# A three-layer CIN on one core: VectorE makes X_1 ahead of T3_1 in the second pairs, chunk 4's factor moves behind T3_0, the first pairs' squarings behind a copy

## The chip, the cores and the metric

The kernel runs on one core of a Trainium2 chip. Its time is in device microseconds (us), the median of three runs. A profile is one execution, taken by the hardware profiler; its times count from the span's start. Engines: PE (TensorE), with its weight loads as PEld; DVE (VectorE); ACT (ScalarE); POOL (GpSimd); SP, which issues loads.

## The reference

A compressed interaction network over `x` of shape 1024 x 64 x 16 (rows, fields f, elements e), all in float32:

```python
x0 = x; h = x
for i in range(3):
    z = einsum('bfe,bge->bfge', x0, h).reshape(B, 64 * 64, 16)
    y = einsum('oc,bce->boe', W[i], z) + b[i][None, :, None]     # W[i]: 128 x 4096
    x_i, h = (y[:, :64], y[:, 64:]) if i < 2 else (y, y)
    xs.append(x_i)
out = sum(concatenate(xs, axis=1), axis=2) @ fc_w.T + fc_b        # 1024 x 1
```

Only one number per row leaves it, so the kernel folds the third layer and the sums into products of pairs of fields with small weight matrices made at the start. What is left per row and element is a set of contractions of all products `x_f * x_g`.

## The kernel before

**Chunks and quarters.** The 1024 rows are 32 chunks of 32 rows; a chunk is 512 columns (32 rows x 16 elements). For chunk c, `xa_c` holds `x` on 128 partitions in 4 rotations i, `xb_c_j` holds it in quarter j of 4 further rotations. The product of the two (128 x 4 x 512, a block of 2048 columns) holds a quarter of the field pairs. Fourteen such blocks (`z`) lie in SBUF; `take` and `used` (lines 87 to 96) hand them out in the order in which they come free, worked out when the program is built.

**Pairs.** Chunks 0 to 5 are done singly. Chunks 6 to 31 are done two at a time, as pairs n = 0 to 12 (k = 3 to 15), each of a chunk a and a chunk b. A pair is one 2 x 2 block product done with seven multiplications in place of eight, so that sums of products stand in for some of them. VectorE makes, for j = 0 and 1 (`make_pair`, line 694; `w_product`, line 640):

- B22_j: `xa_b` times quarter j + 2 of b;
- a small sum in place (`w_both`, line 646): quarter j of b is added into the PSUM bank that holds quarter j + 2;
- T3_j: `xa_b` times that sum, from the same PSUM bank;
- X_j: `xa_a` times quarter j of a;
- B21_j: `xa_a` times quarter j + 2 of a.

Each product but T3 has a quarter that ScalarE first copies into a PSUM bank (`second`, line 554); there are two such banks, used in turn. GpSimd then mixes (`w_mix`, line 651): T2 from X and T3, later others; for j = 1 T2 is written over X in place (line 654), in two halves. One mix of each pair is an accumulating DMA.

**TensorE.** It multiplies the products and mixes with weights of 64 columns (`mm`, line 527). Two matmuls lie side by side on the two halves of the array's columns, so that a pair of them goes at a time. Four sums per pair stay in PSUM: alpha, beta, gamma (the other half of alpha's bank) and delta. The banks of alpha and delta come from four banks with the tag `acc`, used in turn; before them the sums of chunks 4 and 5 lie there too, so pair 1's alpha and delta take the banks of chunks 4 and 5.

**Order.** Nothing is scheduled by a planner at run time. Every operation is entered in a list with a time by hand (`at(when, fn, ...)`, line 518). Sorted by that time, the list gives the order of each engine's queue; semaphore waits follow from the data and from the reuse of buffers. A pair's window begins at `t = T0 + 31 * n` (line 914); one unit is two matmuls side by side, about 0.86 us. For pairs 1 and later the ten numbers handed to `make_pair` (line 928) are the times, from t, of B22_0, the sum, T3_0, X_0, B22_1, the sum, T3_1, X_1, B21_0 and B21_1; a quarter's copy is entered 2.7 units ahead of its product (line 709). The next seven are GpSimd's mixes.

In odd pairs (`a_leads`, line 785) the window of TensorE opens with X_1 (into alpha) beside T3_0 and then T3_1 (into delta). In even pairs (`o_leads`, line 798) it opens in another order. Even pairs have `joint` 0 (the last one 2), odd ones 1 (line 909).

**Other parts that the change touches.** `factors(c)` (line 287) closes the single chunks 4 and 5: ScalarE scales half of the chunk's sum (line 291), VectorE multiplies it with the other half (line 298). Chunk 4's is entered at T0 + 11, chunk 5's at T0 + 25.3 (line 900); these times lie in pair 0's window. `square(c)` (line 179) squares a chunk on ScalarE; `load_pair` (line 829) enters the two squarings of a pair 10 units into its window (line 839). `load_pair` also enters the loads on SP: `xa` has three slots, so that a chunk's load waits until the last product that reads the slot's old chunk is done.

Of the kernel before, what the change touches and what calls it, by code (L numbers as in the profile page):

```python
# [70 lines left out]
def cin_kernel(ctx, tc, xra, xrb, wh, w0r, w1h, w2t, wx1, wx0, vec, lin, out):  # L71
# [298 lines left out]
    for h in range(2):  # L370
        at = slice(32 * h, 32 * h + 32)
# [146 lines left out]
    def at(when, fn, *args, **flags):  # L518
        ops.append((when, len(ops), fn, args, flags))
# [174 lines left out]
    def make_pair(t, p, when, mixed):  # L694
        a, b = p["a"], p["b"]
        for when, c, j, name, uses in (
            (when[0], b, 2, "B22", 5), (when[1], b, 0, None, 0), (when[2], b, 0, "T3", 9),
            (when[3], a, 0, "X", 5), (when[4], b, 3, "B22", 5), (when[5], b, 1, None, 0),
            (when[6], b, 1, "T3", 9), (when[7], a, 1, "X", 13 if p["k"] > 3 else 5), (when[8], a, 2, "B21", 5),
            (when[9], a, 3, "B21", 5),  # L700
        ):
            if name is None:
                at(t + when, w_both, p, j)
                continue
            if name == "B21" and j == 2 and p["k"] == 3:
                at(t + when, w_product, p, c, j, name, uses, engine=nc.gpsimd)
                continue
            if name != "T3":
                ahead = 3.3 if p["k"] > 4 and name == "B22" and j == 2 else 2.7
                if p["k"] == 3 and name == "X" and j == 1:  # L710
                    ahead = 9.1
                at(t + when - ahead, second, c, j)
            at(t + when, w_product, p, c, j, name, uses)
        t2, t1, t4 = ("T2", "X", "T3"), ("T3", "B22", "T2"), ("T2", "T2", "B21")
        for when, j, names in zip(
            mixed, (0, 1, 1, 0, 1, 1, 0), (t2, (*t2, 0, 2), (*t2, 2), t1, t1, t4, t4)
        ):
            if names == t4 and j and p["k"] % 2:
                at(t + when - 1.5, w_mix, p, j, *names, 0, 2)
                names = (*t4, 2)  # L720
            at(t + when, w_mix, p, j, *names)
        at(t + 29, lambda: used(p["B21"][p["k"] % 2 ^ 1]))
# [51 lines left out]
    def first_window(t, p, after, left):  # L774
        window(
            t, p,
            p1_run(p, GROUPS) + left[1][:1] + [(q_extra, 4, va)] + w_run(p, alpha, s2, "T2")
            + left[1][1:] + w_run(p, alpha, s1, "T3"),
            p7_run(p, GROUPS) + left[0][:1] + [(q_extra, 5, va)]
            + w_run(p, beta, wq_all, "B21", True, 2 * NI) + left[0][1:]  # L780
            + p1_run(after, FIRST_ROW) + p4_run(p)[:-LATE],
            8, 8, 18,
        )
# [29 lines left out]
    def end_pair(t, p, whens):  # L813
        hb_, qa, uub, ha, uua, xv, add = whens
        at(t + hb_, w_hb, p)
        at(t + qa, w_qa, p)
        at(t + uub, w_uu, p, alpha, "A", snaps[2])
        at(t + ha, w_ha, p)
        at(t + uua, w_uu, p, delta, "O", snaps[0])
        if p["joint"] == 0:  # L820
            at(t + uub - 0.1, w_hb_squares, p)
        if p["joint"] == 1:
            at(t + xv, x_v0x_parts, p)
        else:
            at(t + xv, x_v0x, p["k"])
        at(t + add, sums, p["k"])


    def load_pair(t, p, b0, a0, b1, a1):
        a, b = p["a"], p["b"]  # L830
        at(t + b0, load_xa, b)
        at(t + b0, load_xb, b, 2, 0)
        at(t + a0, load_xa, a)
        at(t + a0, load_xb, a, 0)
        at(t + b1, load_xb, b, 3, 1)
        at(t + a1, load_xb, a, 1, 2, 3)
        for c in (b, a):
            at(t + 1, load_e, c)
            at(t + 10, square, c)
        at(t + 1.1, load_xx, p["k"])  # L840


# [54 lines left out]
    for c in (0, 1):  # L897
        at(34.5, factors, c)
    at(34.6, sums, 0, slice(0, 128), slice(0, 1))
    for c, when in ((4, 11), (5, 25.3)):  # L900
        at(T0 + when, factors, c)
    at(T0 + 29.1, sums, 2, slice(0, 128), slice(0, 1))

# [9 lines left out]
    for n, p in enumerate(pairs):  # L913
        t = T0 + SPAN * n
        q, after = pairs[n - 1], pairs[n + 1] if n + 1 < NPAIR else None
        if n == 0:
            load_pair(t, p, -39.9, -33.3, -39.8, -27)
            make_pair(
                t, p, (-23.4, -20.7, -20.4, -16.5, -17.2, -16.8, -16.6, -7, -13.5, 3),
                (-14, -6.9, -6.8, 7.2, 12.4, 17.6, 15.9),  # L920
            )
            first_window(
                t, p, after, [[(contract_half, 5, 3, i, h) for i in (2, 3)] for h in range(2)]
            )
        else:
            load_pair(t, p, -34, -28, -27.8, -27.7)
            make_pair(
                t, p, (-21.4, -18.7, -18.4, -15.8, -12.2, -9.5, -6.1, -2, 1.6, 4.2),
                (-5, 1.6, 3.6, 7.2 if n % 2 else 0.2, 12.4, 18.6, 18.5 if n % 2 else 16.9),
            )  # L930
            (a_leads if n % 2 else o_leads)(t, p, q, after)
            if n % 2:
                end_pair(t, q, (0.7, 11.7, 21.2, 22.3, 23.2, 21.3, 36))
            else:
                end_pair(t, q, (0.7, 11.7, 17.9, 22.3, 23.2, 17.8, 36))
# [36 lines left out]
    t, q = T0 + SPAN * NPAIR, pairs[-1]  # L972
# [184 lines left out]
```

## Time and profile before

| | us |
|---|---|
| median of three runs (447.61 to 448.14) | 447.92 |
| the profiled execution, its own time | 447.98 |
| its span, first to last instruction | 446.2 |
| TensorE busy | 441.4 |
| VectorE busy | 403.6 |
| GpSimd busy | 367.5 |
| ScalarE busy | 116.9 |
| products at L642 on VectorE, 103 | 231.2, 2.28 each |
| mixes at L659 on GpSimd, 85 | 300.7, 3.57 each (4.55 a whole block, 2.4 a half) |
| windows of pairs 0, 1, 2, 3 begin on TensorE at | 84.3, 109.2, 136.2, 161.2 |

The granted clock of TensorE is 1.00 throughout. The profile's lines hold, for a group of instructions, line, engine, operation, output <- input, count, then busy time and the mean of one in ns, then the idle time before them and what ended most of it. In a timeline a line has start, length, engine, line, operation, and in brackets the idle time before it with the releaser. `PEld alpha L528 <- DVE z L642` in the list of waits reads: a weight load for a matmul into alpha stood until VectorE's product of line 642 was done. Matmul ends are modelled, so idle time of TensorE is read from the starts.

### The profile page before, as it was taken

The page shows a single profiled execution, that of the slowest core. Times are in us where ns is not written, and L with a number is a line of the kernel's source. Part 1 is how long each engine was busy: PE and PEld are TensorE (multiplying, and loading weights), DVE is VectorE, ACT ScalarE, POOL GpSimd, SP SyncE. Part 2 cuts the span into 40 slices and gives each one's busy share as a digit, 9 for nine tenths or more (in the row PEclk, how much of TensorE's full clock was granted, in tenths as well). Part 3 has the DMA queues.
Part 4 walks back from the last instruction along what each step waited for, and adds up shares of the span by engine and source line. Part 5 has one row for each costly group of instructions (what it writes and reads, how often), then busy time and mean ns, then how long its engine had stood idle before and what let it go on. Part 6 is the DMA issues. An engine that isn't in the chain of part 4 may idle for free.

```text
span 446.2 us, 5956 instructions
## 1 busy us (share of the span) xinstructions
PE 441.4 (99%) x2234; PEld 153.4 (34%) x2234; DVE 403.6 (90%) x305; ACT 116.9 (26%) x215; POOL 367.5 (82%) x135
## 2 busy tenths in 40 slices
PE   9999999999999999999999999999999999999997
PEld 5333333334333333333333333333333333333345
DVE  4996899979998999989999999989999899999744
ACT  2263341232313223131312223131231313123211
POOL 5424788998998979899798979989798997989900
PEclk9999999999999999999999999999999999999999
DMA  8997996399649775796929877497747968492400
GB/s 304 414 337 191 374 410 266 86 354 246 258 106 312 207 239 176 169 356 138 325 84 235 295 203 269 115 326 184 255 166 176 352 138 326 129 271 64 95 1 0
DMA packets 35060, 99.85 MB, mean 224 GB/s; under 512 B 6388, under 2 KB 7188, under 8 KB 28440
## 3 DMA queue, kind: packets, MB, share of 16 engines
q1 hardware_dynamic: 31560, 84.70, 54.0%
q0 software_dynamic: 1872, 13.63, 16.7%
q10 hardware_dynamic: 1600, 1.15, 1.1%
q8 instruction: 17, 0.28, 0.3%
q14 instruction: 11, 0.09, 0.1%
HBM read 84.20 MB, written 1.64 MB: 192 GB/s over the span
## 4 chain that ended last, share of the span: by engine, by line
PE 88%; DMA 6%; DVE 4%; issue 1%; ACT 1%; SPq 0%; DVEq 0%
PE alpha L528 40%; PE delta L528 22%; PE beta L528 11%; PE acc L528 6%; PE q L528 3%; DMA xa<-in_xra 3%; PE acc L281 3%; DVE z L642 2%; DMA xb<-in_xrb 2%; PE acc L248 2%; DMA z<-in_w0r 1%; DVE z L240 1%; PE y L528 0%; DVE uu L298 0%; DVE xp L648 0%
## 5 line engine op out<-in xcount | busy, mean ns | idle before, releaser
L659 POOL TENSOR_TENSOR z<-z,z 128x2048 f32<-128x2048 f32 (+1 forms) x85 | 300.7, 3571 | 25.5 <-PE alpha L528 14.8
L642 DVE TENSOR_TENSOR z<-xa,xp 128x2048 f32<-128x2048 f32 x103 | 231.2, 2280 | 3.0 <-ACT xp L556 1.8
L528 PE MATMUL alpha<-z,ws 128*64 128x512 f32 x624 | 233.1, 593 | 0.0
L528 PEld LDWEIGHTS alpha<-z,ws 128*64 128x64 f32 x624 | 72.9, 137 | 91.5 <-issue 86.4
L528 PE MATMUL delta<-z,w_all 128*64 128x512 f32 x208 | 96.4, 592 | 0.0
L528 PE MATMUL alpha<-z,w_all 128*64 128x512 f32 x208 | 92.7, 593 | 1.0 <-DVE z L642 1.0
L528 PE MATMUL beta<-z,w_all 128*64 128x512 f32 x208 | 91.7, 594 | 0.0
L528 PE MATMUL delta<-z,ws 128*64 128x512 f32 x208 | 91.7, 594 | 0.0
L556 ACT COPY xp<-xb 128x512 f32<-128x512 f32 x88 | 51.3, 585 | 134.4 <-DVE z L642 113.4
L240 DVE TENSOR_TENSOR z<-xa,xp 128x2048 f32<-128x2048 f32 (+1 forms) x29 | 45.5, 1620 | 3.6 <-ACT xp L556 2.2
L240 POOL TENSOR_TENSOR z<-xa,xb 128x2048 f32<-128x2048 f32 x6 | 27.3, 4570 | 17.1 <-DMA xb<-in_xrb 17.0
L528 PEld LDWEIGHTS alpha<-z,w_all 128*64 128x64 f32 x208 | 28.0, 137 | 33.3 <-issue 26.0
L528 PEld LDWEIGHTS delta<-z,w_all 128*64 128x64 f32 x208 | 28.5, 137 | 30.4 <-issue 29.7
L528 PEld LDWEIGHTS beta<-z,w_all 128*64 128x64 f32 x208 | 28.0, 137 | 27.4 <-issue 25.7
L528 PEld LDWEIGHTS delta<-z,ws 128*64 128x64 f32 x208 | 28.0, 137 | 27.4 <-issue 25.7
L528 PE MATMUL acc<-z,w_all 128*64 128x512 f32 x128 | 28.1, 592 | 0.0
L673 ACT ACTIVATE snap<-alpha,vs 64x512 f32<-64x512 f32 x13 | 8.9, 682 | 49.8 <-PE alpha L528 49.8
L248 PE MATMUL acc<-z,w_all 128*64 128x512 f32 x96 | 21.6, 598 | 0.3 <-DVE z L240 0.3
L305 DVE TENSOR_REDUCE acc<-uu 128x64 f32<-128x1024 f32 (+2 forms) x19 | 19.6, 1036 | 0.2
L676 ACT COPY snap<-delta 64x512 f32<-64x512 f32 x13 | 7.5, 581 | 42.6 <-PE alpha L528 28.3
L648 DVE TENSOR_TENSOR xp<-xp,xb 128x512 f32<-128x512 f32 x26 | 18.1, 697 | 0.6
L670 ACT COPY snap<-alpha 64x512 f32<-64x512 f32 x13 | 7.6, 581 | 39.9 <-PE delta L528 25.6
(130 smaller groups left out, 369.1 us busy)
## 6 DMA issues: line engine op xcount, KB each, us to landing
xa<-in_xra SPq DMA_DIRECT2D x32, 1024.0 KB, 5.8
xb<-in_xrb SPq DMA_DIRECT2D x128, 256.0 KB, 6.9
z<-z POOLq DMA_DIRECT2D x13, 1024.0 KB, 8.1
e<-in_xra SPq DMA_DIRECT2D x28, 128.0 KB, 7.0
xx<-in_xra SPq DMA_DIRECT2D x28, 128.0 KB, 2.6
z<-in_w2t SPq DMA_DIRECT2D x2, 1024.0 KB, 8.7
z<-in_wx SPq DMA_DIRECT2D x2, 1024.0 KB, 10.4
xa<-in_xra SPq DMA_DIRECT2D x5, 256.0 KB, 4.0
```

The source lines that it names most:

```text
L240: engine.tensor_tensor(blocks[zs[c, j]][:, at, :], xas[c][:, at, :], xbs[c][j].unsqueeze(1).to_broadcast([128, last - first, N]), ALU.mult,)
L248: nc.tensor.matmul(accs[c][halves[i % 2]], w_all[:, j * NI + i, 0:64], blocks[zs[c, j]][:, i, :], start=(j == 0 and i < 2), stop=(j == las ...
L281: nc.tensor.matmul(accs[c][halves[1 - c % 2]], w_all[:, t, 64:128], blocks[zs[c, j]][:, i, :], start=(t == 0), stop=False, skip_group_chec ...
L305: nc.vector.tensor_reduce(acc[rows, of, k, half], uu[rows, of if at is None else at, E * half.start : E * half.stop].rearrange("p k (b e) ...
L528: nc.tensor.matmul(out, w, rhs, start=start, stop=stop, skip_group_check=True)
L556: nc.scalar.copy(bank, xbs[c][j])
L642: engine.tensor_tensor(blocks[b], xas[c], xbs[c][j].unsqueeze(1).to_broadcast([128, NI, N]), ALU.mult)
L648: nc.vector.tensor_tensor(bank, bank, xbs[p["b"]][j], ALU.add)
L659: nc.gpsimd.tensor_tensor(*(blocks[b][:, first:last] for b in (o, x, y)), ALU.subtract if in1 == "T3" else ALU.add,)
L670: nc.scalar.copy(snaps[0][p["O"]], alpha(p))
L673: nc.scalar.activation(snaps[1][p["O"]], alpha(p), AF.Identity, bias=bh1[p["A"]])
L676: nc.scalar.copy(snaps[2][p["A"]], delta(p))
```

## The change

Three times in the list of operations are changed. No operation is added or taken away.

```diff
@@ load_pair @@
         for c in (b, a):
             at(t + 1, load_e, c)
-            at(t + 10, square, c)
+            at(t + (10 if p["joint"] == 1 else 14), square, c)
         at(t + 1.1, load_xx, p["k"])
@@ the single chunks 4 and 5 @@
-    for c, when in ((4, 11), (5, 25.3)):
+    for c, when in ((4, 12.7), (5, 25.3)):
         at(T0 + when, factors, c)
@@ pairs 1 and later @@
             load_pair(t, p, -34, -28, -27.8, -27.7)
             make_pair(
-                t, p, (-21.4, -18.7, -18.4, -15.8, -12.2, -9.5, -6.1, -2, 1.6, 4.2),
+                t, p, (-21.4, -18.7, -18.4, -15.8, -12.2, -9.5, -6.1, -6.2 if n % 2 else -2, 1.6, 4.2),
                 (-5, 1.6, 3.6, 7.2 if n % 2 else 0.2, 12.4, 18.6, 18.5 if n % 2 else 16.9),
             )
```

- In odd pairs ("second pairs") X_1 is entered at -6.2, just ahead of T3_1 at -6.1, instead of -2; its quarter's copy on ScalarE moves with it, to -8.9. On VectorE the two products change places. As blocks are handed out in the order of the list, X_1 and T3_1 also get other blocks than before.
- Chunk 4's factor is entered at T0 + 12.7, which is behind pair 1's T3_0 (T0 + 12.6); its scaling on ScalarE moves with it, behind the copy for pair 1's X_0 (T0 + 12.5).
- In even pairs ("first pairs") the two squarings are entered 14 units into the window instead of 10, behind the copy for the next pair's X_0 (12.5 units in).

Chunk 5's factor keeps its time, T0 + 25.3. That is 5.7 units ahead of pair 1's window: behind T3_1, and before the change ahead of X_1, after it behind X_1.

## The prediction

> **What bounds the kernel now.** I read the shares of busy time first, then the list of waits, then the timelines of the places that the waits point at. The page gives, engine by engine, busy time, share of the span and instructions:
>
> ```profile
> PE 441.4 (99%) x2234; PEld 153.4 (34%) x2234; DVE 403.6 (90%) x305; ACT 116.9 (26%) x215; POOL 367.5 (82%) x135
> ```
>
> TensorE is the bound, so only time in which it stands still can be won. A matmul record of 512 columns is followed by the next one of its column half 0.43 us later, two halves side by side; I looked for larger steps. From 84 us on there are only two kinds: around the matmuls on squares (64 rows; 0.53, 0.48 and 0.54, 0.48 us), which the change leaves alone, and at the start of the odd pairs' windows. The list of waits has the second kind (total, times, longest, in us; two groups of the same wait):
>
> ```profile
> PEld alpha L528 <- DVE z L642: 6.4, 7, 1.8
> ...
> PE alpha L528 <- DVE z L642: 1.0, 1, 1.0
> ```
>
> One is long, six are short. The long one is pair 1's start, in TensorE's timeline:
>
> ```profile
> 107.44 0.59 PE L528 MATMUL delta<-z,w_all 128*64 128x512 f32 x1
> 107.65 0.59 PE L528 MATMUL alpha<-z,ws 128*64 128x512 f32 x1
> 109.20 0.64 PE L528 MATMUL alpha<-z,w_all 128*64 128x512 f32 x1 [0.96 <-DVE z L642]
> ```
>
> The next two matmuls were due at 107.87 and 108.08 and both start at 109.20. What they wait for is in VectorE's timeline:
>
> ```profile
> 103.74 2.29 DVE L642 TENSOR_TENSOR z<-xa,xp 128x2048 f32<-128x2048 f32 x1
> 106.06 0.76 DVE L298 SCALAR_TENSOR_TENSOR uu<-acc,vs,snap 64x512 f32<-64x512 f32 x1
> 106.85 2.29 DVE L642 TENSOR_TENSOR z<-xa,xp 128x2048 f32<-128x2048 f32 x1
> ```
>
> These are T3_1, chunk 5's factor and X_1. X_1 ends at 109.14 and TensorE starts 0.06 later. T3_1, made first, is first read four matmul pairs later, at 112.69. Pair 3's start shows the short kind:
>
> ```profile
> 160.63 0.59 PE L528 MATMUL delta<-z,w_all 128*64 128x512 f32 x1
> 160.64 0.59 PE L528 MATMUL alpha<-z,ws 128*64 128x512 f32 x1
> 161.17 0.64 PE L528 MATMUL alpha<-z,w_all 128*64 128x512 f32 x1
> 161.18 0.64 PE L528 MATMUL delta<-z,ws 128*64 128x512 f32 x1
> 161.65 0.59 PE L528 MATMUL alpha<-z,w_all 128*64 128x512 f32 x1
> ```
>
> A step of 0.54 and one of 0.48 in place of 0.43 each; T3_1 and X_1 lie together on VectorE from 156.63 to 161.12, X_1 last, and TensorE starts 0.05 after it.
>
> **A rule that speaks against a gain here.** The steps at 161 look like those around the squares (123.41 to 123.94, then 0.48), where the tile form goes from 128*64 to 64*64. The Trainium skill, TensorEngine Tiling (Array Packing), Key Properties, says that a change of tiling mode drains TensorE; were the short steps such drains, the 0.81 us below would stay and the sum would be 447.06. The row decides against it: the form is 128*64 on both sides at 161, the even pairs' starts (188.14 to 188.57, 0.43) show no step at the same place, and X_1's end stands 0.05 before the start all five times.
>
> **The change part by part.**
>
> *Pairs 3, 5, 7, 9, 11: X_1 and T3_1 change places on VectorE.* Nothing is added. Both take 2.28, so X_1 ends at 158.92 instead of 161.12 and T3_1 at 161.12. The start is then free: the five steps are 0.541, 0.540, 0.535, 0.544 and 0.541, less 0.429 each: 0.56; the five second steps of 0.48 give 5 x 0.051 = 0.25. Together **0.81 us**. What is late next:
> - T3_1 on TensorE is wanted at 164.66, 3.5 after its end. GpSimd's mix of X_1 and T3_1 starts at 163.18 and is held by TensorE's reading of X_1 (idle 2.65, released by alpha), not by T3_1.
> - The block that T3_1 now takes was last read by GpSimd's half mix that ends at 155.88; VectorE comes at 158.9. Spare: 3.
> - The PSUM bank of T3_1's operand is copied over for the next product (B21_0). That copy started at 158.95, now at 161.15; 0.59 later it is there, at 161.74. VectorE is covered until 162.03 by the sum at L680 (161.28, 0.76). Spare: 0.3, so 0.
> - SP's queue: the load of the next pair's chunk a into the slot that T3_1 read was issued at 158.95, now at 161.15, with six quarter loads behind it. At the medians in this stretch (4.7 us to landing for a chunk, 6.9 for a quarter) the chunk lands at 165.9, its first quarter at 168.5; the readers come at 173.44 (VectorE) and 169.97 (ScalarE). Spare: 1.5 or more, so 0.
> - The next tightest products for TensorE over the whole run have 1.7 us to spare, in the even pairs.
>
> *Pair 1: the same swap, and chunk 4's factor behind T3_0.* Before, VectorE stands 2.55 us idle until 94.69, because the factor waits for ScalarE's scaling (94.06), and that for the two squarings in front of it (92.89 to 94.04). After, step by step from 92.14, where the product before ends: sum 0.70, T3_0 2.28, factor 0.75, X_0 2.28, B22_1 2.28, sum 0.70, with some 0.1 between: 101.2. X_1 then needs its quarter copied by ScalarE, which sits behind the copy at L673 (100.36, 0.68, released by TensorE): ready at 101.65. X_1 runs to 104.0, 4 us before it is due. T3_1 cannot follow at once: its new block is the one that pair 0's B21_1 held (the order of both programs with their waits shows a wait for GpSimd), and GpSimd reads that until the second half of this row:
>
> ```profile
> 100.13 9.57 POOL L659 TENSOR_TENSOR z<-z,z 128x1024 f32<-128x1024 f32 x3
> ```
>
> (two halves, 100.13 to 105.08, and a product). So T3_1 runs 105.15 to 107.43. Chunk 5's factor is queued behind it, and lands at 108.22. **Here a wait is added**: the window's second matmul, the first into delta, writes the PSUM bank that chunk 5's factor reads. Before, the factor was done ahead of X_1, so that the wait for X_1 covered it; in the changed program this matmul waits for VectorE itself. It starts at 108.22 + 0.06 = 108.28 against 108.08 due: 0.20 of stall takes the place of 1.12. Behind it stands all of TensorE's queue, but the other half runs on until its own next matmul at 108.73, as the halves did 0.2 apart before 107.87. Gain **0.92 us**. Bounds: 1.17 if GpSimd's block is free earlier and nothing waits (1.12 and the second step's 0.05); 0, if chunk 5's factor comes as late as X_1 did. I take 0.92, since each duration in it is a row. VectorE then reaches B21_0 at 109.7 instead of 110.56; GpSimd's next mix, which waited 1.51 for TensorE at 111.21, starts at about 109.7.
>
> *The even pairs' squarings, four units later, and chunk 4's scaling on ScalarE.* ScalarE is 26% busy. At 143.86 the two squarings (0.62 each) stand in front of the copy for X_0 (144.91), and X_0 starts at 147.78; the squares are read at 164.65 and later. 0 either way, with 2 us of cover on one side and 19 on the other.
>
> Sum against the profiled execution's own time of 447.98 (span 446.2 and 1.8 around it): 447.98 - 0.81 - 0.92 = 446.25. The median of the runs shown is 447.92, 0.06 lower; by it 446.2. To the end of the kernel nothing takes the gain back: the last window's products have 10 us and more to spare, and TensorE runs without a step from 423 on.
>
> **Rivals.**
> 1. *The short steps stay* (another wait comes within 0.1 of X_1's, or a restart that no row names). Only pair 1 pays: 447.98 - 0.92 = 447.06. For: the steps are small, and I know only that X_1's end fits. Against: no other product ends within 1.7 us.
> 2. *Pair 1's stall only changes its name*: T3_1 is held longer by GpSimd and chunk 5's factor comes at 109.1. Only the odd pairs pay: 447.17. For: VectorE has nothing else to do in that place and GpSimd's spans are rough. Against: GpSimd's chain up to 105.08 is the same program, without idle time.
> 3. *Nothing*: both hold, 447.9. The program does do what it says: in the order of the changed kernel X_1 stands ahead of T3_1 in all six odd pairs.
> 4. *Slower*: B21_0's copy. It can start only when T3_1 ends. Place: VectorE at 162.0 in the six odd pairs. It costs nothing until it is 0.3 late (the sum's cover) and then 1.7 more (the spare of the even pairs' X_1); past 2.0 us each further one costs one, six times. For 0.2% slower, 448.8, it would need (448.8 - 446.25) / 6 = 0.43 past that point; at 0.55 past it, 449.5. Against: ScalarE is idle from 153.99 to 158.95, with nothing ahead of the copy.
>
> **How the numbers follow.** Both gains: 0.71, own range 445.7 (pair 1's 1.17, and 0.3 for the spread of the median; the runs shown lie 0.5 apart) to 446.8. Short steps stay 0.11; pair 1's stall stays 0.08; nothing 0.05; slower 0.05. The range takes in the first two rivals: 445.7 to 447.2, which leaves about 0.1 outside, and spread. Faster than 447.92 by over 0.2% (about what a measurement here can tell from no change) means below 447.02: all of the first, half of rival 1, a third of rival 2: 0.79. Same: the rest of those and rival 3: 0.16. Slower 0.05.
>
> **What would show it.** In the changed kernel's waits, alpha's wait for the product at L642 falls from 6.4 us to the plain 0.3 each; the five starts step by 0.43. At pair 1's start the wait names L298, on delta, and is about 0.2. VectorE's 2.55 idle before L298 is gone, and T3_1 of pair 1 stands idle for GpSimd about 1 us. The starts of pairs 3, 5, 7, 9, 11 come every 51.8 us instead of 51.97. Wrong would be: a step at a pair's start with another releaser, or ScalarE's copies released later than the sum at L680 ends.

## The result, and the profile after

The changed kernel takes 445.48 us (median of 6 runs, 445.25 to 446.4) against 447.97 of the kernel before (6 runs, 447.59 to 448.49): a ratio of 0.9947 [0.9934, 0.996], 2.49 us less. The forecast was 446.2 with a range of 445.7 to 447.2. The sign and both mechanisms were right; the gain was 2.49 in place of 1.73, and the time lies 0.22 below the range.

The profiled execution is the slowest of the six: 446.40, span 444.6, granted clock 1.00. Its own gain, 447.98 - 446.40 = 1.58, is less than forecast. So the profile has to be read with care: it shows what went from pair 1 on, and something else that differs from execution to execution.

The page of the changed kernel, first part:

```profile
PE 440.5 (99%) x2234; PEld 154.0 (35%) x2234; DVE 403.5 (91%) x305; ACT 117.3 (26%) x215; POOL 367.4 (83%) x135
```

TensorE is still the bound. Its list of waits (total, times, longest, in us) has three lines on the products of line 642 and on line 298 that matter here:

```profile
DVE z L642 <- POOL z L659: 1.1, 1, 1.1
...
PEld alpha L528 <- DVE z L642: 0.3, 1, 0.3
...
PEld delta L528 <- DVE uu L298: 0.2, 1, 0.2
```

Alpha's waits for products of line 642 have fallen from 6.4 us in seven times and 1.0 in one to 0.3 in one, and that one stands at 138.39, in pair 2's window, not at an odd pair's start. (Of the seven, six were for X_1; the seventh, 0.45 at 100.73, lay in pair 0's window, so the prediction's "six are short" counts one too many.) What has come instead is the new wait that the forecast named, on delta, for chunk 5's factor. VectorE waits once 1.1 for GpSimd's block. TensorE's timeline at pair 1's start:

```profile
107.83 0.59 PE L528 MATMUL alpha<-z,ws 128*64 128x512 f32 x1
108.05 0.59 PE L528 MATMUL alpha<-z,w_all 128*64 128x512 f32 x1
108.42 0.64 PE L528 MATMUL delta<-z,ws 128*64 128x512 f32 x1
```

X_1 is no longer waited for: alpha starts at 108.05, 0.22 after the matmul before, as the halves did ahead of it. Delta was due 0.21 later, at 108.26, and starts at 108.42. VectorE's timeline says why:

```profile
101.93 2.29 DVE L642 TENSOR_TENSOR z<-xa,xp 128x2048 f32<-128x2048 f32 x1 [0.67 <-ACT xp L556]
105.29 2.29 DVE L642 TENSOR_TENSOR z<-xa,xp 128x2048 f32<-128x2048 f32 x1 [1.07 <-POOL z L659]
107.61 0.76 DVE L298 SCALAR_TENSOR_TENSOR uu<-acc,vs,snap 64x512 f32<-64x512 f32 x1
```

X_1, then T3_1 held by GpSimd, then chunk 5's factor, which ends at 108.37; TensorE follows 0.05 later. GpSimd's timeline shows the two halves and the whole-block mix behind them in one row (the prediction calls the third operation of this row a product; line 659 is a mix):

```profile
100.40 9.34 POOL L659 TENSOR_TENSOR z<-z,z 128x1024 f32<-128x1024 f32 x3
```

The halves end at 105.26, and T3_1 starts 0.03 later. Pair 3's start on TensorE has no short step left (159.85 to 160.28 is 0.43, as everywhere):

```profile
159.85 0.59 PE L528 MATMUL delta<-z,w_all 128*64 128x512 f32 x1
159.86 0.59 PE L528 MATMUL alpha<-z,ws 128*64 128x512 f32 x1
160.28 0.59 PE L528 MATMUL alpha<-z,w_all 128*64 128x512 f32 x1
```

**Where the time went.** I set the starts of the same matmuls of the two profiles against each other, by their place in TensorE's queue. Ahead of pair 1 the changed kernel is 0.18 *later*, from 43 to 101 us and by the same amount throughout. Behind pair 1's start, once the two column halves run level again, it is 0.78 earlier; behind the two steps of the starts of pairs 3 to 11 it is 0.94, 1.10, 1.26, 1.43 and 1.59 earlier, and 1.59 at the end. So the part of the kernel that the change touches won 1.59 + 0.18 = 1.77 us, against a forecast of 1.73, and an unchanged part, ahead of 43 us, lost 0.18. The other five runs must have been earlier in that part, or have won more in the touched one. That is the open question.

### The profile page after: what moved, and what is told of

Same layout as the page of the kernel before. It is cut to its first block, busy times and chain, and to the rows that moved or that the text cites. A ratio compares the mean times of both kernels' runs of the same rounds, so it can differ in the third digit from the quotient of the medians.

```text
span 444.6 us, 5946 instructions
## 1 busy us (share of the span) xinstructions
PE 440.5 (99%) x2234; PEld 154.0 (35%) x2234; DVE 403.5 (91%) x305; ACT 117.3 (26%) x215; POOL 367.4 (83%) x135
## 4 chain that ended last, share of the span: by engine, by line
PE 91%; DMA 6%; DVE 1%; SPq 0%; issue 0%; DVEq 0%
PE alpha L528 42%; PE delta L528 23%; PE beta L528 10%; PE acc L528 7%; PE q L528 3%; DMA xa<-in_xra 3%; PE acc L281 3%; DMA xb<-in_xrb 2%; PE acc L248 2%; DMA z<-in_w0r 1%; DVE z L240 1%; PE y L528 0%; SPq L145 0%; SPq L195 0%; PE hx L528 0%
```

## The experiments

**Theory.** Two separate things were removed: chunk 4's factor behind T3_0 takes away the stall of pair 1, the swap takes away the short steps of pairs 3 to 11. What lies beyond them is scatter of the start-up, and has nothing to do with the change. **Rivals:** the swap alone, or the squarings, did what the factor is credited with; or the changed kernel really starts earlier, by a mechanism that the forecast missed.

For each run two numbers come from the profile: the *start-up*, how much later the matmul that stood at 43.18 in the first profile of before starts, and what was *won* between there and the end. 447.98 plus the first less the second gives every profiled execution's own time within 0.05 us, so what lies outside these two (behind the last matmul, and around the span) hardly varies. In `e3` and `e4` the two column halves stand 0.03 apart at that place; the later one is taken. The names in brackets are those by which the text calls the runs.

| run | median us (runs) | before, beside it | ratio | start-up | won | own time |
|---|---|---|---|---|---|---|
| the changed kernel, first | 445.48 (6) | 447.97 | 0.9947 [0.9934, 0.996] | +0.18 | 1.77 | 446.40 |
| again (`e1_again`) | 445.56 (5) | 447.86 | 0.9948 [0.9936, 0.9961] | -0.75 | 1.98 | 445.25 |
| again (`e6_after`) | 445.88 (5) | 447.79 | 0.9958 [0.9946, 0.9971] | +0.01 | 1.98 | 446.00 |
| again (`e9_after`) | 445.38 (1) | 447.77 | | -0.64 | 1.99 | 445.38 |
| swap only (`e2`) | 446.39 (6) | 447.86 | 0.9967 [0.9955, 0.9979] | +0.33 | 1.17 | 447.18 |
| no swap (`e5`) | 446.56 (7) | 447.86 | 0.9971 [0.996, 0.9982] | 0.00 | 1.21 | 446.80 |
| factor 4 only (`e8`) | 446.83 (11) | 447.79 | 0.9978 [0.9969, 0.9987] | +0.02 | 1.20 | 446.84 |
| squarings only (`e7`) | 447.30 (11) | 447.77 | 0.9993 [0.9984, 1.0002] | -0.20 | 0.52 | 447.27 |
| chunk 5's factor ahead too (`e3`) | 445.87 (5) | 447.86 | 0.9955 [0.9942, 0.9967] | -0.07 | 1.99 | 445.93 |
| swap not in pair 1 (`e4`) | 445.79 (5) | 447.79 | 0.9958 [0.9944, 0.9971] | +0.21 | 1.98 | 446.20 |
| before against itself (`b1`) | 447.91 (11) | 447.79 | 1.0002 [0.9994, 1.0011] | -0.06 | 0.02 | 447.91 |
| before, one profile (`b2`) | 447.92 (1) | 447.77 | | -0.03 | 0.03 | 447.92 |

### The changed kernel again

No edit.

> The changed kernel once more, for a second profile. Its first profiled execution took 446.40, its other five 445.25 to 445.66. Theory A (the gain is the stalls of TensorE and nothing else: 0.81 at the odd pairs' starts and about 0.95 at pair 1's, 1.77 by the first profile; the rest is scatter ahead of the pairs): median 446.2, and a profile whose windows from 84 us on are the same as in the first, whatever its time. Theory B (the first profiled execution was an unlucky one: in most executions pair 1's start has no stall at all and something more is saved): median 445.5, and a profile of that time whose pair 1 starts without the 0.37 step and that is shorter from 84 us on too.

The time repeats: 445.56, ratio 0.9948. The profile does not. The start-up is 0.75 earlier than in the first profile of before, and at pair 1 TensorE waits for nothing: GpSimd's halves end at 103.89, T3_1 runs 103.92 to 106.21, chunk 5's factor ends at 107.0, and delta starts at 107.33, 0.21 behind alpha and on time. 1.98 is won. This is theory B for pair 1's start; what goes beyond it in the time is the start-up, which is not in theory B. Both the stall that the first profile showed at pair 1 and its start-up belong to that execution, not to the kernel.

### The swap alone

```diff
-p, (-21.4, -18.7, -18.4, -15.8, -12.2, -9.5, -6.1, -2, 1.6, 4.2),
+p, (-21.4, -18.7, -18.4, -15.8, -12.2, -9.5, -6.1, -6.2 if n % 2 else -2, 1.6, 4.2),
```

> X_1 ahead of T3_1 in the odd pairs alone; chunk 4's factor and the squarings stay where they were before. Theory A: VectorE keeps its 2.55 us of idle time ahead of chunk 4's factor, so X_1 of pair 1 ends at 106.0, T3_1 at 108.3 and chunk 5's factor at 109.1; the first matmul into delta starts at 109.17 against 109.20 before, nothing won there; the five short steps go. 0.84 faster than before, 447.1. Theory B: as much as the changed kernel, 445.5 to 446, if the swap carries the whole gain.

All five short steps are gone, and in pair 1 the wait only changes its name. VectorE's timeline, X_1 and T3_1 in one row and then chunk 5's factor:

```profile
95.02 0.74 DVE L298 SCALAR_TENSOR_TENSOR uu<-acc,vs,snap 64x512 f32<-64x512 f32 x1 [1.69 <-ACT snap L291]
...
103.85 4.48 DVE L642 TENSOR_TENSOR z<-xa,xp 128x2048 f32<-128x2048 f32 x2
108.36 0.76 DVE L298 SCALAR_TENSOR_TENSOR uu<-acc,vs,snap 64x512 f32<-64x512 f32 x1
```

and TensorE's:

```profile
108.20 1.02 PE L528 MATMUL alpha<-z,w_all 128*64 128x512 f32 x2
109.17 0.64 PE L528 MATMUL delta<-z,ws 128*64 128x512 f32 x1
```

Chunk 4's factor still stands idle for ScalarE ahead of everything, the queue behind it is late, and delta starts 0.05 after chunk 5's factor ends (109.12): 0.76 past the 108.41 due. The swap alone wins 1.17: 0.81 in the five starts and 0.36 at pair 1. The expectation had nothing at pair 1: its 109.17 for delta came as put, but in an execution that was 0.33 later from the start. Less this start-up, VectorE is through with X_1, T3_1 and the factor 0.35 earlier than before (109.12 against 109.14). The median, 446.39, lies 1.47 below before, 0.3 more than was won; the profiled run is the slowest of its six. The outcome at pair 1 is that of rival 2 of the forecast (the wait changes its name), though what holds it is VectorE's late queue and not GpSimd.

### The factor and the squarings without the swap

```diff
-            at(t + 10, square, c)
+            at(t + (10 if p["joint"] == 1 else 14), square, c)
-    for c, when in ((4, 11), (5, 25.3)):
+    for c, when in ((4, 12.7), (5, 25.3)):
```

> Chunk 4's factor and the squarings moved as in the change, X_1 left behind T3_1. Theory A: the factor's move alone takes 2.2 us of idle time off VectorE ahead of pair 1, X_1 ends at 106.7, before 107.87 when it is due, so pair 1's stall of 1.12 goes wholly, and the short steps of 0.16 at pairs 3, 5, 7, 9 and 11 stay: 1.1 to 1.2 faster than before, 446.8. Theory B (the swap carries the gain): as before, 447.9.

Pair 1's start is free and the short steps are all there (0.53 each). TensorE's timeline at pair 1 and pair 3:

```profile
107.87 0.59 PE L528 MATMUL alpha<-z,w_all 128*64 128x512 f32 x1
108.08 0.59 PE L528 MATMUL delta<-z,ws 128*64 128x512 f32 x1
...
159.45 0.59 PE L528 MATMUL delta<-z,w_all 128*64 128x512 f32 x1
159.46 0.59 PE L528 MATMUL alpha<-z,ws 128*64 128x512 f32 x1
159.99 0.64 PE L528 MATMUL alpha<-z,w_all 128*64 128x512 f32 x1
```

Alpha and delta start at 107.87 and 108.08, the very times at which the forecast had them due. Pair 1's whole stall, 1.18 with the step behind it, goes with the factor and without the swap. The swap's worth is then what it does to the five starts.

### Chunk 4's factor alone

```diff
-    for c, when in ((4, 11), (5, 25.3)):
+    for c, when in ((4, 12.7), (5, 25.3)):
```

> The kernel before with chunk 4's factor behind pair 1's T3_0 and nothing else: the squarings stay 10 units into the window. Theory A (the factor's place alone takes VectorE's idle 2.55 away, since T3_0 then lies in front of it; the squarings cost nothing either way): ScalarE's scaling ends near 95.2, where T3_0 ends on VectorE; the stall of 1.12 at pair 1 is gone with the 0.05 behind it, the five steps of 0.54 stay, 447.9 - 1.17 = 446.7, equal to the run with factor and squarings moved (446.56). Rival (both moves are needed, as the squarings stand in front of the scaling): a stall of 0.3 to 1.1 stays at pair 1, 447.0 to 447.9.

ScalarE's timeline and VectorE's:

```profile
92.91 1.15 ACT L180 ACTIVATE e<-e 64x512 f32<-64x512 f32 x2
94.00 0.59 ACT L556 COPY xp<-xb 128x512 f32<-128x512 f32 x1
94.61 0.59 ACT L291 ACTIVATE snap<-acc 64x512 f32<-64x512 f32 x1
```

```profile
92.91 2.29 DVE L642 TENSOR_TENSOR z<-xa,xp 128x2048 f32<-128x2048 f32 x1
95.24 0.74 DVE L298 SCALAR_TENSOR_TENSOR uu<-acc,vs,snap 64x512 f32<-64x512 f32 x1
```

The squarings still stand in front of the scaling, which ends at 95.20, where T3_0 ends on VectorE too; the factor starts 0.04 later and nothing is lost. 1.20 is won, the same as with the squarings moved (1.21), and the time is 446.83 with 446.7 expected. The squarings add nothing once the factor is moved.

### The squarings alone

```diff
-            at(t + 10, square, c)
+            at(t + (10 if p["joint"] == 1 else 14), square, c)
```

> The kernel before with the squarings of even pairs at 14 in place of 10 units and nothing else: chunk 4's factor stays in front of VectorE's T3_0, but ScalarE's scaling is no longer behind the two squarings. The scaling then waits for chunk 4's last matmul (93.27 to 93.3 in the kernel before) and ends near 93.9 in place of 94.65, so that the factor and all of VectorE behind it come 0.76 earlier. Theory A (the squarings and the factor's place are two cures for one wait; with the factor moved the squarings are worth nothing): X_1 of pair 1 ends 108.4, TensorE starts at 108.45 against 107.87 and 108.08 due, a stall of 0.36 is left, the gain is 0.76 and the time 447.0 to 447.1. Rival (as the forecast priced them, 0 by themselves): 447.8.

The two lines to read are ScalarE's scaling and VectorE's factor:

```profile
93.37 0.59 ACT L291 ACTIVATE snap<-acc 64x512 f32<-64x512 f32 x1 [0.58 <-ACT snap L676]
...
94.00 0.74 DVE L298 SCALAR_TENSOR_TENSOR uu<-acc,vs,snap 64x512 f32<-64x512 f32 x1 [1.60 <-ACT snap L291]
```

Less the start-up of 0.20 the factor comes 0.49 earlier than before, not 0.76. The releaser named for the scaling is ScalarE's copy, which had ended at 92.79; by the program it reads chunk 4's sum, and the last group of matmuls of that sum starts at 92.21 and ends (modelled) at 93.24 on TensorE, 0.13 before the scaling starts. 0.52 is won, the right mechanism with a price 0.25 too high. By the times alone (447.30, ratio up to 1.0002) it can't be told from no change; by the profile it can. So the squarings are a weaker cure for the same wait. The forecast's 0 for them holds only beside the moved factor.

### Chunk 5's factor ahead of T3_1 as well

On top of the change:

```diff
-    for c, when in ((4, 12.7), (5, 25.3)):
+    for c, when in ((4, 12.7), (5, 24.85)):
```

> The changed kernel with chunk 5's factor between X_1 and T3_1 (24.85 units in place of 25.3), so that the added wait at pair 1's start goes. Theory A: the 0.37 step at pair 1's start becomes 0.21 or nothing (the halves as far apart as before it), 0.2 to 0.4 faster than the changed kernel. Theory B (no stall there in most executions): same as the changed kernel within 0.1.

VectorE's order is now X_1, chunk 5's factor, T3_1: the factor ends at 104.76, and delta no longer stands behind T3_1's wait for GpSimd. 1.99 is won; the median, 445.87, is not the 0.2 to 0.4 less of theory A, but 0.31 more than the changed kernel's beside it (445.56), within the spread of the runs.

### The swap everywhere but in pair 1

On top of the change:

```diff
-... -6.2 if n % 2 else -2, 1.6, 4.2),
+... -6.2 if n % 2 and n > 1 else -2, 1.6, 4.2),
```

> The change with X_1 and T3_1 left in their old order in pair 1 alone (pairs 3 to 11 as in the changed kernel). Theory A (the two parts are the moved factor, worth 1.17 at pair 1 by itself, and the five starts, worth 0.81; at pair 1 the swap adds nothing and leaves a wait of 0 to 0.37 on chunk 5's factor): no stall at pair 1, no step at the other five starts, 1.98 won in the profile, the median at 445.5 to 445.9, equal to the changed kernel's or up to 0.2 less in the same runs. Rival (the swap is what frees pair 1 as well): a stall is left at pair 1 and the time is 446.3 or more.

1.98 won, no stall at pair 1 (108.08 and 108.29), no short step later, 445.79. At pair 1 the swap adds nothing to the moved factor. Neither of these two versions beats the changed kernel by what a measurement can tell; what they remove is a wait that comes in some executions only.

### The changed kernel a third time

> The changed kernel once more, a third profile and a third set of times. Theory A (the start-up's scatter): the time is 445.3 to 446.0, the part won from pair 1 on is again 1.77 to 1.98 (1.59 or more at the steps that were there, no other), and the profile's start-up lies anywhere within 1 us of the first one's. Theory B (an earlier start-up belongs to the change): its matmuls at 43 to 101 us stand 0.5 or more ahead of the kernel before, as in the second profile and not as in the first.

445.88, 1.91 less than before in the same runs, 1.98 won, start-up +0.01. The lines at pair 1, GpSimd's, then VectorE's (X_1 and T3_1 in one row), then TensorE's:

```profile
99.21 9.45 POOL L659 TENSOR_TENSOR z<-z,z 128x1024 f32<-128x1024 f32 x3
```

```profile
101.76 4.71 DVE L642 TENSOR_TENSOR z<-xa,xp 128x2048 f32<-128x2048 f32 x2 [0.73 <-ACT xp L556]
106.50 0.76 DVE L298 SCALAR_TENSOR_TENSOR uu<-acc,vs,snap 64x512 f32<-64x512 f32 x1
```

```profile
107.88 0.59 PE L528 MATMUL alpha<-z,w_all 128*64 128x512 f32 x1
108.09 0.59 PE L528 MATMUL delta<-z,ws 128*64 128x512 f32 x1
```

GpSimd's row begins 1.19 earlier than in the first profile while TensorE stands only 0.17 earlier. The halves end at 104.15, T3_1 waits 0.1 instead of 1.07, and chunk 5's factor is done 0.8 before delta wants its bank. The earlier start-up of the second profile is not there, so it does not come with the change every time.

### The kernel before against itself

> The kernel before, unchanged, against itself. Open is where the part of the gain comes from that the five starts and pair 1's start do not hold (they hold 1.77 in the changed kernel's first profile and 1.98 in its second, of 2.4 to 2.5). Theory A (the start-up scatters by itself from execution to execution, whatever the changed lines): the ratio is 1.000 within 0.0015, and this second profile of the kernel before can have its matmuls between 43 and 101 us up to 1 us earlier or later than the first one, with the same steps afterwards (1.12 at pair 1, 0.541 five times). Theory B (the changed kernel really starts earlier, since its executions free the loads' slots or queues at other times): the ratio is 1.000 too, but the profile has its matmuls at 43 us within 0.1 of the first one's.

Ratio 1.0002 [0.9994, 1.0011]; the steps are those of the first profile. Its start-up is within 0.06 of the first one's, which is what the rival of an earlier start expects, and no evidence against scatter. GpSimd's second half at pair 1, however, ends at 103.40 here and at 105.08 in the first profile, with TensorE at the same place within 0.06. Where GpSimd gets this from stands 33 us earlier in its timeline, first in the first profile of before, then in this one:

```profile
72.15 4.57 POOL L539 TENSOR_TENSOR z<-z,vs 128x2048 f32<-128x2048 f32 x1 [1.19 <-DMA z<-in_wx]
```

```profile
70.36 4.57 POOL L539 TENSOR_TENSOR z<-z,vs 128x2048 f32<-128x2048 f32 x1 [0.47 <-DMA z<-in_wx]
```

GpSimd waits there for the load of a weight block, and from there to the halves it hardly stands idle. In all thirteen profiles this operation waits for that load (0.24 to 1.23), starts at 70.36 to 72.36, and the second half at pair 1 ends 32.90 to 33.04 after its start. So by these figures, whether delta has to wait at pair 1 in the changed kernel hangs on when one load lands.

### One more profile of each

> One more look at the changed kernel, for the scatter of two places. GpSimd's second half in pair 1 ended at 105.26, 103.89 and 104.15 in three profiles; theory: this execution has it between 103.4 and 105.3, and the first matmul into delta is late by its end + 4.27 (T3_1 2.3, chunk 5's factor 0.8 and the gaps) less the time due, if that is positive. Its matmul 90 of TensorE starts between 42.4 and 43.5, the bounds of ten profiles of one start-up.

GpSimd's halves end at 103.90 and TensorE doesn't wait for them. (The figure of 4.27 in the expectation is a slip: T3_1, the factor and the gaps make 108.42 - 105.26 = 3.16, by which delta would be ready at 107.06, and it was due at 107.44.) The start-up is 0.64 earlier.

> One more look at the kernel before, for the scatter of the same two places: GpSimd's second half in pair 1 (105.08 and 103.40 so far) between 103.4 and 105.3, while X_1 of pair 1 ends at 109.1 whatever it is; TensorE's matmul 90 (43.17 and 43.12 so far) between 42.4 and 43.5 if the start-up scatters by itself, within 0.1 of 43.15 if it belongs to this kernel.

GpSimd's half ends at 104.07. The start-up is 0.03 from the first profile's, which by the expectation's own words (within 0.1 of 43.15) speaks for the rival; but on the way it was not: at 12 us TensorE stands 0.68 earlier than in the first profile of before, and loses that again by 31. This run shows what makes a start-up. TensorE's timeline of the first profile of before, then of this one:

```profile
4.04 3.26 PE L218 MATMUL xp<-xa,shift 64*64 64x512 f32 x16
```

```profile
4.20 1.95 PE L218 MATMUL xp<-xa,shift 64*64 64x512 f32 x16 [0.23 <-DMA xa<-in_xra]
```

The same sixteen matmuls, four at a time, step by 0.85 in the one and by 0.43 in the other. VectorE's products (line 240) follow them, so they come early as well, until one meets a load. VectorE's timeline, in the same order:

```profile
22.05 2.29 DVE L240 TENSOR_TENSOR z<-xa,xp 128x2048 f32<-128x2048 f32 x1
24.26 2.28 DVE L240 TENSOR_TENSOR z<-xa,xb 128x2048 f32<-128x2048 f32 x1
```

```profile
21.37 2.29 DVE L240 TENSOR_TENSOR z<-xa,xp 128x2048 f32<-128x2048 f32 x1
24.22 2.29 DVE L240 TENSOR_TENSOR z<-xa,xb 128x2048 f32<-128x2048 f32 x1 [0.56 <-DMA xb<-in_xrb]
```

VectorE is 0.68 early, waits 0.56 for a quarter of `x`, and is where the first profile had it. From there on seven such products run without a gap, and TensorE's matmul at 43 starts 18.91 to 18.93 after that product in twelve of the thirteen profiles (19.16 in `e4`). In the fourth profile of the changed kernel the load is there in time:

```profile
23.62 2.28 DVE L240 TENSOR_TENSOR z<-xa,xb 128x2048 f32<-128x2048 f32 x1
```

No wait, 0.64 earlier, and 445.38. So the start-up is the later of two things: VectorE's own chain, and the landing of one quarter. The pace of TensorE's first steps moves that chain but does not set it alone: in `e6_after` VectorE is 0.27 early at 15.2 us, waits 0.62 for TensorE at line 363 (0.32 in the first profile of before), and starts its product at 22.07.

## Why the prediction was right or wrong

**The bound, right.** TensorE at 99% in all profiles, and every gain is a step of TensorE that got shorter.

**The odd pairs, right: 0.81 forecast, 0.81 measured.** The won time grows from 0.96 behind pair 1's start to 1.77 in the changed kernel's first profile, from 1.18 to 1.98 or 1.99 in the others, and from 1.18 (no swap) to 1.98 or 1.99 (swap added). Nothing was late next: GpSimd, the copy for B21_0 and the loads left no step on TensorE. With this, rivals 1, 3 and 4 fall.

**The rule on tiling modes.** The steps of 0.54 and 0.48 at the pairs' starts are gone with a mere change of order on VectorE, while those round the squares, where the form changes from 128*64 to 64*64 and back, are still there (in `e6_after` 0.53 and 0.48, then 0.54 and 0.48, in each of the windows that have squares). So the drain that the Trainium skill, TensorEngine Tiling (Array Packing), Key Properties, describes fits the second kind and not the first; no run here takes the change of form away to test it. A start that follows a wait by a tenth of a microsecond looks the same in the steps; only the form of the matmuls on both sides and the end of the product it waits for told them apart.

**Pair 1, right in mechanism, mis-sized: 0.92 forecast; 0.96 in the first profile, 1.18 in the other three.** Each row of the forecast came as put, X_1 off the path, T3_1 held by GpSimd to 105.26 (105.08, to which this start-up adds 0.18), the factor's end at 108.37 (108.22 and 0.18 make 108.40), the new wait on delta. But the step by which T3_1 starts only behind GpSimd's half, at 105.08, took GpSimd's place from one execution. In thirteen profiles of this part the second half ends at 105.08 to 105.26 three times and at 103.40 to 104.33 ten times, for TensorE at the same place within 1.1. What varies is not the length of a GpSimd row but the landing of a load 33 us before, which the sum took for fixed. The bound of 1.17 was in the range, but it was the usual case and not the end. The sum for the usual case was 447.98 - 0.81 - 1.18 = 446.0.

**The squarings, right beside the factor, wrong by themselves:** 0 with it (1.20 against 1.21), 0.52 without it.

**The median, the step that failed.** The sum was set against one profiled execution's own time, with 0.3 "for the spread of the median" at the lower end; that took the start-up for all but fixed. It rested on three runs of before that lie 0.5 apart; the 66 on record lie 1.4 apart. In thirteen profiles of one and the same code ahead of 92 us it lies between 42.43 and 43.51, 1.08 apart. The first comparison's runs fell on the early side (445.25 to 445.66 in five of six): with 1.98 won, its median stands for a start-up near -0.5, and 0.3 did not cover that. Of the 2.49, 1.8 to 2.0 were won by the change; the rest, by this sum, is the start-up of those runs. That is worked out and not seen, as five of the six have no profile. The comparison's own interval, 0.9934 to 0.996, is 1.8 to 3.0 us and has 1.98 in it; the other two comparisons give 2.30 and 1.91.

**What stays open.** The four profiles of the changed kernel have two early start-ups and the three of before none; over all 16 timed runs up to the third comparison the changed kernel's median is 445.61, 2.2 below that of the 39 of before (447.81), 0.2 more than the profiles' 1.98. The instruction lists of both kernels are the same in kind and order on every engine up to 92.9 us, where the squarings stood on ScalarE, so I can name nothing in the change that could do it, and the six kernels that share parts of it start at 42.98 to 43.51. Two more figures speak for scatter: those 66 runs of the kernel before lie between 447.10 and 448.49, so it too has executions 0.9 ahead of its first profile; and `e3` and `e4`, which win the same 1.98 with another order at pair 1, have a median of 445.86 in ten runs, 1.95 below the 447.81 of those 66. But seven profiles are too few to exclude that 0.2.

## What to carry to other kernels

When a product that is wanted first stands behind one that is wanted later, look at the operation that makes the whole queue late too: here moving one small operation behind a product (factor 4 behind T3_0) covered its wait for another engine and won 1.2 us, 0.4 more than reordering five windows.

Two cures for one wait don't add: price each by itself and both together. And before a sum is made against one profiled execution, ask which of its terms differ between executions of the same code; at gains of half a per cent, the start-up and the place of an unhurried engine (here set by the landing of one load 33 us before) belong in the range.

## What the runs showed of the hardware

- **TensorE's first matmuls run at half pace for a time that differs between executions.** The first three steps at line 218 take 0.85 to 0.91 each, or 0.43 to 0.50 each, or begin with the one and go over to the other. All three are slow in five of the thirteen profiles, none in four, and in the rest it changes over in between, after 4.8 to 6.6 us of the span. The granted clock in the profile's rows is 1.00 in these stretches in both cases, so it doesn't show this; the steps do.
- **A stop of TensorE costs more than its length.** A start that came 0.11 late was followed by a step of 0.48 instead of 0.43, at the five pairs' starts, after the 0.16 on delta in the changed kernel (108.42, then 108.90) and after the 1.12 at pair 1 before (109.20, then 109.68): 0.05 on top each time.
- **The releaser of a wait can be the wrong one by half a microsecond.** ScalarE's scaling in `e7` is put down to a copy that had ended 0.58 before; the last matmul of the sum that it reads ends 0.13 before it starts.
